# A larger pad ahead of q's pool, and one raw q buffer, in a self-attention kernel

## Chip, cores and metric

One core of a Trainium2 chip. The metric is device microseconds of one execution, the median over several executions. An interval is a 95% interval.

## The reference, cut to what matters

```python
def _L0_conv_ref(x, Wq, bq, Wk, bk, Wv, bv, gamma):      # x: (4, 64, 64, 256) float32
    q = jnp.einsum('bwhc,cd->bwhd', x, Wq) + bq           # 128 columns
    k = jnp.einsum('bwhc,cd->bwhd', x, Wk) + bk
    v = jnp.einsum('bwhc,cd->bwhd', x, Wv) + bv           # 256 columns
    pq = q.reshape(B, -1, N); pk = k.reshape(B, -1, N); pv = v.reshape(B, -1, N)   # N = 4096
    energy = jnp.einsum('bcn,bcm->bnm', pq, pk)
    attention = jax.nn.softmax(energy, axis=-1)
    out = jnp.einsum('bcm,bnm->bcn', pv, attention)
    return gamma * out.reshape(B, W, H, C) + x
```

There are four images, each with a 4096 x 4096 attention. The kernel splits operands into parts of type fp32r and forms each product from three matmuls.

## The kernel before

Per image the main loop has 128 steps, `u`, in 16 groups of eight. `t` is the step's number in its group. A step runs 12 energy matmuls on TensorE (`sa`, `sa`, `sb`, four times), and then 8 matmuls each with `vh`, `vl` and `vd`. All of them have 128x128 weights and a moving operand of 256 or 258 columns. "bb" below is the product with `vd` and `d`.

```python
xpool, xtpool, qkv = pool("xpool", 3), pool("xtpool", 3), pool("qkv", 1)

pool("pad", 1).tile([P, 16], F32, name="pad")      # 64 bytes a partition
ppool = pool("ppool", 2)                           # x, y, h, l, d
pool("pad2", 1).tile([P, 16], F32, name="pad2")    # 64 bytes: the change is here
work, kpool = pool("work", 2), pool("kpool", 3)    # work: raw q ("qr"), q, o ...; kpool: k
...
vh = qkv.tile([P, NM, VC], F32R, tag="vh", name="vh")   # VC = 260: rows of 1040 bytes
vl = qkv.tile([P, NM, VC], F32R, tag="vl", name="vl")
vd = qkv.tile([P, NM, C], F32R, tag="vd", name="vd")    # rows of 1024 bytes
...
def load_q(b, g):
    t = work.tile([P, NJ, P], F32, tag="qr", name=f"qr_{b}_{g}")
    nc.sync.dma_start(t, qd[b, g])
    loads[b, "qr", g] = t
...
# energy(b, u, k), called for k = 0 and 1
for i in range(2):
    for to, f, first, last in ((sa, 0, True, False), (sa, 1, False, True), (sb, 2, True, True)):
        nc.tensor.matmul(to[:, i], kt[:, 2 * k + i, f, :], q[:, f], start=first, stop=last)
...
# attend(b, u)
for left, right in ((h, vh), (l, vl), (d, vd)):
    for j in range(NJ):
        out_ = bb[:, j, :] if left is d else acc[j]
        for i in range(4):
            m = 2 * t + i // 2 + NI * (i % 2)
            nc.tensor.matmul(out_, left[:, i, j * P : (j + 1) * P], right[:, m, : out_.shape[1]], ...)
```

The first operand given to `matmul` is the stationary one (the weights: k, h, l, d), the second the moving one (q, vh, vl, vd).

## Time and profile before

| | before |
|---|---|
| median of the first three runs | 2494.41 us (2494.12 to 2496.48) |
| PE busy, weight loads busy | 99%, 98% |
| spacing, energy matmuls | 117 to 119 ns in most steps |
| spacing, bb matmuls | about 120 falling to 113 ns within the eight |

A *spacing* is the time from the start of one matmul to the start of the next. It is taken from the start times, in nanoseconds, that the trace holds for every matmul. The rows of the page give durations instead, and those overlap. The prediction shows the page's rows and the timeline.

### The profile page before, as it was taken

To read this page: it belongs to the slowest core of one execution; us is meant where nothing else is said; L and a number is where in the kernel's file an instruction comes from. 1 tells how busy PE (TensorE), PEld (TensorE's weight loads), DVE (VectorE), ACT (ScalarE), POOL (GpSimd) and SP (SyncE) were. 2 spreads that over 40 slices of the span, in tenths; PEclk is the share of its full clock that TensorE was granted. 3 is DMA by queue.
4 is the path that set the end of the run, shared out by engine and by line. 5 is a ranking of instruction groups with operands and counts; after the bars stand their busy time and mean duration, and the time that the engine had idled before them with its cause. 6 is when DMAs were issued, how large, how long until landed. Compare 5 with 4: busy or idle time off the path is not lost.

```text
span 2494.6 us, 50085 instructions
## 1 busy us (share of the span) xinstructions
PE 2481.1 (99%) x19982; PEld 2438.4 (98%) x19982; DVE 2106.9 (84%) x2440; ACT 1809.1 (73%) x3138; POOL 425.7 (17%) x780
## 2 busy tenths in 40 slices
PE   9999999999999999999999999999999999999998
PEld 8999999999899999999989999999998999999998
DVE  5888888888698888888869888888886988888887
ACT  5777777777677777777667777777766777777775
POOL 4211111111411111111041111111114111111110
PEclk9999999999999999999999999999999999999999
DMA  7666666664766666666477666666648666666663
GB/s 231 222 195 210 201 201 200 198 202 156 235 220 193 206 199 203 206 188 208 139 244 223 197 193 209 201 208 195 191 145 253 217 201 196 203 203 207 199 193 110
DMA packets 137408, 498.92 MB, mean 200 GB/s; under 512 B 15536, under 2 KB 57264, under 8 KB 137168
## 3 DMA queue, kind: packets, MB, share of 16 engines
q0 software_dynamic: 92320, 453.17, 58.0%
q1 hardware_dynamic: 44304, 42.22, 5.7%
q8 instruction: 160, 2.62, 0.4%
q14 instruction: 80, 0.66, 0.1%
q10 hardware_dynamic: 544, 0.26, 0.0%
HBM read 445.25 MB, written 50.33 MB: 199 GB/s over the span
## 4 chain that ended last, share of the span: by engine, by line
PE 95%; ACT 2%; DVE 1%; issue 1%; DMA 1%; POOL 0%; SPq 0%; ACTq 0%; DVEq 0%; POOLq 0%
PE a L370 38%; PE sa L320 19%; PE bb L370 18%; PE sb L320 10%; PE qk L136 4%; PE v L157 4%; PE ot L416 1%; PE xt L123 1%; ACT h L339 1%; DVE x L334 1%; ACT x L324 0%; ACT y L324 0%; ACT vh L284 0%; DMA kf<-f 0%; DVE vd L287 0%
## 5 line engine op out<-in xcount | busy, mean ns | idle before, releaser
L324 ACT ACTIVATE x<-sa 128x512 f32<-128x512 f32 x1024 | 609.4, 595 | 398.3 <-PE sa L320 330.0
L320 PE MATMUL sa<-q,k 128*128 128x256 f32 x4096 | 757.4, 283 | 1.4 <-ACT x L324 0.9
L334 DVE TENSOR_TENSOR x<-x,y 128x1024 f32<-128x1024 f32 x512 | 625.9, 1222 | 155.6 <-ACT y L324 155.6
L320 PEld LDWEIGHTS sa<-q,k 128*128 128x128 f32 x4096 | 625.7, 189 | 2.8 <-ACT x L324 1.7
L345 DVE TENSOR_TENSOR l<-x,h 128x1024 fp32r<-128x1024 f32 x512 | 624.6, 1220 | 0.0
L348 DVE SCALAR_TENSOR_TENSOR d<-h,x 128x1024 fp32r<-128x1024 f32 x512 | 624.5, 1220 | 0.0
L324 ACT ACTIVATE y<-sb 128x512 f32<-128x512 f32 x1024 | 613.2, 599 | 0.0
L320 PE MATMUL sb<-q,k 128*128 128x256 f32 x2048 | 582.0, 284 | 0.0
L370 PE MATMUL a<-vh,h 128*128 128x258 f32 x4096 | 578.3, 284 | 0.0
L339 ACT ACTIVATE h<-x 128x1024 fp32r<-128x1024 f32 x512 | 543.7, 1062 | 43.1 <-DVE x L334 38.3
L370 PE MATMUL a<-vl,l 128*128 128x258 f32 x4096 | 573.3, 282 | 0.0
L370 PE MATMUL bb<-vd,d 128*128 128x256 f32 x4096 | 557.3, 278 | 0.0
L304 POOL DMA_DIRECT2D k<-kf x512 | 280.5, 548 | 1485.6 <-PE sb L320 1467.0
L370 PEld LDWEIGHTS a<-vh,h 128*128 128x128 f32 x4096 | 526.3, 190 | 0.0
L370 PEld LDWEIGHTS a<-vl,l 128*128 128x128 f32 x4096 | 526.2, 190 | 0.0
L370 PEld LDWEIGHTS bb<-vd,d 128*128 128x128 f32 x4096 | 514.1, 188 | 0.0
L320 PEld LDWEIGHTS sb<-q,k 128*128 128x128 f32 x2048 | 384.5, 188 | 9.4 <-ACT y L324 1.4
L136 PE MATMUL qk<-wqk_sb,xts 128*128 128x256 f32 x512 | 122.8, 383 | 0.0
L400 DVE SCALAR_TENSOR_TENSOR o<-a,o 128x256 f32<-128x256 f32 x126 | 47.6, 420 | 86.9 <-ACT o L380 86.9
L157 PE MATMUL v<-xts,wv_sb 128*128 128x256 f32 x512 | 120.3, 379 | 0.0
L157 PEld LDWEIGHTS v<-xts,wv_sb 128*128 128x128 f32 x512 | 97.3, 190 | 13.2
L408 ACT ACTIVATE o<-o,r 128x256 f32<-128x256 f32 x126 | 57.6, 505 | 72.4 <-DVE r L391 72.4
(54 smaller groups left out, 931.0 us busy)
## 6 DMA issues: line engine op xcount, KB each, us to landing
k<-kf POOLq DMA_DIRECT2D x512, 768.0 KB, 4.8
x<-in_x_dram SPq DMA_DIRECT2D x128, 256.0 KB, 3.6
kf<-f POOLq DMA_DIRECT2D x64, 384.0 KB, 3.8
out_dram<-x POOLq DMA_DIRECT2D x63, 256.0 KB, 2.5
qd<-qks POOLq DMA_DIRECT2D x128, 64.0 KB, 3.0
qr<-qd SPq DMA_DIRECT2D x64, 128.0 KB, 3.0
wv_sb<-in_L_conv_Wv_dram POOLq DMA_DIRECT2D x1, 256.0 KB, 5.7
out_dram<-x SPq DMA_DIRECT2D x1, 256.0 KB, 4.1
```

The lines of the kernel that those rows point to most:

```text
L136: nc.tensor.matmul(qk[:, s, :], self.xt[i][:, k, s, :], wqk_sb[:, k, :], start=(k == 0), stop=(k == KC - 1),)
L157: nc.tensor.matmul(vp[:, eh, :], wv_sb[:, k, eh * P : (eh + 1) * P], self.xt[i][:, k].rearrange("p s a -> p (s a)"), start=(k == 0), stop= ...
L304: nc.gpsimd.dma_start(t.rearrange("p (i s) f d -> p i s (f d)", s=2), kf[b, u % NU])
L320: nc.tensor.matmul(to[:, i], kt[:, 2 * k + i, f, :], q[:, f], start=first, stop=last)
L324: nc.scalar.activation(to[:, 2 * k : 2 * k + 2, :], sp.rearrange("p i j d -> p i (j d)"), AF.Exp, scale=scale,)
L334: nc.vector.tensor_tensor(x, x, y, ALU.mult)
L339: nc.scalar.activation(h, units[b, u], AF.Identity, scale=UPPER)
L345: nc.vector.tensor_tensor(l, x, h.bitcast(F32), ALU.subtract)
L348: nc.vector.scalar_tensor_tensor(d, h.bitcast(F32), 1.0 + E, x, ALU.mult, ALU.subtract)
L370: nc.tensor.matmul(out_, left[:, i, j * P : (j + 1) * P], right[:, m, : out_.shape[1]], start=(t == i == 0 and (left is h or left is d and ...
L400: nc.vector.scalar_tensor_tensor(o[:, j, :], a[:, :C], 1.0 + E, o[:, j, :], ALU.mult, ALU.add)
L408: nc.scalar.activation(o[:, j, :], o[:, j, :], AF.Identity, scale=r[:, j : j + 1])
```

## The change

The pad ahead of q's pool grows from 64 to 448 bytes. Everything after it moves, and q and k come to lie where vd and d lie, modulo 512 bytes: q goes from 416 to 288, k from 480 to 352 (vd is at 288, d at 352). SBUF was full, so the raw q tile loses its second buffer to make room.

```diff
-        pool("pad2", 1).tile([P, 16], F32, name="pad2")
+        pool("pad2", 1).tile([P, 112], F32, name="pad2")
@@
-            t = work.tile([P, NJ, P], F32, tag="qr", name=f"qr_{b}_{g}")
+            t = work.tile([P, NJ, P], F32, tag="qr", name=f"qr_{b}_{g}", bufs=1)
```

No instruction is added, removed or reordered.

## The prediction

> **What bounds the kernel now.** I read the page first, then the timeline of TensorE inside the main loop, and then the start time of every matmul in the trace, which the page's means hide.
>
> The head of the page and three rows of its table of groups (the columns are busy us and the mean ns of one):
>
> ```profile
> PE 2481.1 (99%) x19982; PEld 2438.4 (98%) x19982; DVE 2106.9 (84%) x2440; ACT 1809.1 (73%) x3138; POOL 425.7 (17%) x780
> ...
> L320 PE MATMUL sa<-q,k 128*128 128x256 f32 x4096 | 757.4, 283 | 1.4 <-ACT x L324 0.9
> L320 PE MATMUL sb<-q,k 128*128 128x256 f32 x2048 | 582.0, 284 | 0.0
> L370 PE MATMUL bb<-vd,d 128*128 128x256 f32 x4096 | 557.3, 278 | 0.0
> ```
>
> PE and the weight loads beside it are busy 99% and 98% at full clock, and PE idles almost nowhere: the span is a sum of matmul spacings. The mean of 283 ns is a latency (matmuls are pipelined). What counts is the spacing from one start to the next. Though all three rows have one shape (128x128 weights, 256 columns), bb's duration is 5 ns shorter. The timeline of PE over one step of the loop (a step is 12 energy matmuls "sa, sa, sb", then 8 with vh, 8 with vl and 8 with vd):
>
> ```profile
> 857.95 1.09 PE L370 MATMUL bb<-vd,d 128*128 128x256 f32 x8
> 858.88 0.40 PE L320 MATMUL sa<-q,k 128*128 128x256 f32 x2
> ...
> 860.29 0.89 PE L370 MATMUL a<-vh,h 128*128 128x258 f32 x6
> ```
>
> From 858.88 to 860.29 is 1.41 us for 12 energy matmuls, 117.5 ns each; from 857.95 to 858.88 is 0.93 us for 8 bb matmuls, 116 ns each. In one other kind of step the same 12 take less:
>
> ```profile
> 841.86 0.40 PE L320 MATMUL sa<-q,k 128*128 128x256 f32 x2
> ...
> 843.24 0.53 PE L370 MATMUL a<-vh,h 128*128 128x258 f32 x3
> ```
>
> That is 1.38 us, or 115 ns. With the nanosecond starts I sorted spacings by position in the step and by t, the step's number within its group of eight (t = 0 to 7; 64 groups). In the ordinary steps:
> - Energy, t = 3 to 7: 117, 119, 117, 118, ... and a last 122 or 123: 1418 ns for twelve.
> - Energy, t = 2: 118, 117, 117, 119, 116, 114, then 113 six times: 1382 ns.
> - bb, t = 0 and 2 to 7: starts between 118 and 124 and within four or five matmuls settles at 113. bb at t = 1 does not: it stays at 117 to 118.
> - vh and vl, whose tiles move by 16 bytes modulo 512 from one to the next: 113 to 130, mean about 120.
>
> So the same work has **two rhythms, 113.4 and 117.7 ns**, and holds whichever it is in. Of 1431 bb matmuls that followed a spacing of 113 or 114, 1428 had 113 or 114 again; among energy matmuls 117 and 118 lead to 117 to 119 in all but a few of 3248. The addresses in the built program say why two loops behave alike: vd (moving) lies at 288 modulo 512 and d (stationary) at 352; q lies at 416 and k at 480. Both pairs are 64 apart. In going from bb to energy both addresses jump by 128, and there the fast rhythm is lost (113 becomes 117) in t = 3 to 7, while for t = 2 the jump from the slow rhythm of bb happens to end in the fast one.
>
> **What the Trainium skill says.** "TensorE: Matmul & The Clock Gate", section Back-to-back issue gap, gives N/2.4 + 2.5 ns warm; for N = 256 that is 109.2 ns, an estimate from that page. This trace shows 113.4 at best and 117.7 commonly, so 4 to 9 ns a matmul are on top of it. The same page, Part 2, first step (LDWEIGHTS), says that PE has two independent SBUF read ports and that loading the next weights takes no bandwidth from the running matmul. The trace does not agree: only the addresses differ between 113 and 118 to 125. "SBUF — State Buffer", section on the two separate sides, says that PE does not wait on the other engines' ports. Here it agrees: with ACT idle, bb's spacing is 113.7 ns with DVE busy (528 matmuls) and 113.5 with it idle (210). Its Specifications give 224 KiB a partition, 229,376 bytes: in the built program the tiles end at 229,344 before, so a pad 384 bytes larger fits only if something goes, and that is the second raw q buffer (1,024 bytes); the end is then 228,704.
>
> **The change, part by part.** No instruction is added, removed or reordered on any engine; the built programs differ in addresses and in the waits of DMA issues on SP.
>
> (1) The pad. All of work and kpool moves; q now lies at 288 and k at 352 modulo 512, exactly as vd and d. From bb to energy nothing changes in these residues any more, and from energy to the first vh product the weights stay at 352. Energy should then inherit the rhythm that bb ended in:
> - t = 3 to 7 follow a bb at 113. 12 x 113.4 = 1361 ns for 1418: 57 ns saved a step. Such steps with all twelve energy matmuls in a row: 64 + 64 + 60 + 60 + 60 = 308. 308 x 57 = **17.6 us saved.**
> - t = 2 follows the slow bb of t = 1 and loses its lucky jump: 1418 for 1382, 36 ns x 64 = **2.3 us lost.**
> - t = 0 gains nothing. Its first vh product waits for the accumulator, which is freed by a chain from the end of bb:
>
> ```profile
> 832.82 0.59 ACT L380 COPY o<-bb 128x512 f32<-128x512 f32 x1 [0.65 <-PE bb L370]
> ...
> 833.43 0.76 DVE L400 SCALAR_TENSOR_TENSOR o<-a,o 128x256 f32<-128x256 f32 x2 [1.38 <-ACT o L380]
> ...
> 834.03 1.18 PE L370 MATMUL a<-vh,h 128*128 128x258 f32 x8
> ```
>
> The copy of bb, then the first of two DVE operations (half of 0.76), ends near 833.82; the first vh weights load at 833.97, 58 ns late, and the first spacing is 172 in place of about 117. Faster energy lengthens this wait by what it saves.
> - t = 1 gains nothing before its ninth energy matmul: two spacings of about 220 stand there, 200 ns over the usual, and the matmul starts just after ACT's y has ended (838.35), in a row of ACT work that has run back to back since DVE's r. Same reason.
>
> (2) What follows energy. vh and vl start from another rhythm than before. Their spacings depend on the running phase and on what came before, so they can move either way: I take their mean as unchanged. But bb may now settle otherwise for some t. If it stays slow for one t, then 57 ns of energy and about 20 of bb are lost in some 61 steps, 4.7 us. Before, one t in eight was slow; I count a fifth of the five slots, 5 x 0.2 x 4.7 = 4.7 us. Against that, bb of t = 1 may become fast: 57 + 25 ns in 64 steps, 5.2 us, at 0.4 that is 2.1. Net **2.6 us lost**.
>
> (3) One raw q buffer. load_q now waits for the halving of the group before. A group's load is issued two steps before its halving, so it is issued six steps after the last one, about 25 us, while a load lands in 3.0 us (at most 5.5) and has two steps, 8.5 us. From the third load of the first image on, loads waited for an old halving anyway. Cost: nothing.
>
> Sum: 2494.4 - 17.6 + 2.3 + 2.6 = 2481.7, say **2482 us**.
>
> **The rivals.**
> - *The spacing belongs to the operation, not the address* (energy changes PSUM tile and form with each matmul, bb does not). Then nothing moves: 2494. For it: energy runs at 117.7 in seven kinds of step of eight. Against it: at t = 2 the same alternation runs at 113.
> - *Other engines take it up.* DVE has three operations of 1.22 us in a step of 4.25, ACT about 3.4 us, so an ordinary step has 0.5 us in hand; only t = 0 and 1 lack it, and they are counted as zero. If the shorter steps pushed that limit into t = 2 as well, a third of the gain would go: 2487.
> - *bb falls into the slow rhythm for most t.* Then energy inherits 117.7, and bb itself loses some 20 ns a step: 2495 to 2503. Against it: in nearly all contexts seen, whatever stood before, bb ended at 113; t = 1 is the exception.
> - *bb of t = 1 becomes fast and all others stay:* 2494.4 - 17.6 - 2.9 = 2474.
>
> **Range and chances.** The best rival gives 2474, two or three bad slots give 2489 and the first rival 2494. Runs spread 2.4 us. I take 2473 to 2491. Two per cent is 49.9 us; even all 6144 energy matmuls at 4.3 ns less would give 26, so faster by over 2% has 0.01. Slower by 2% would need 4 ns on nearly every product: 0.02.
>
> **What would show it.** In the changed kernel's profile the sa and sb rows should fall from 283 and 284 towards bb's 278; twelve energy matmuls at t = 3 to 7 should take 1.36 us in the timeline; bb should stay near 278; the wait at t = 0 should grow by some 50 ns; qr's rows should show no new idle time of PE or DVE. If sa and sb stay at 283, the address idea falls. If they fall but a<-vh, a<-vl or bb rise, the gain went into other rhythms.

## The result, and the profile after

| | before | after |
|---|---|---|
| median | 2495.38 us (2494.12 to 2496.48, 4 runs) | 2483.40 us (2478.62 to 2484.47, 4 runs) |
| ratio | | 0.9948 (0.9931 to 0.9966) |

A ratio is the mean time of one kernel's runs over that of the other's of the same rounds, so it is not quite the ratio of the medians. The gain is half a per cent, clear of the noise and small.

The page of the changed kernel, its head and the rows of the five products in the loop:

```profile
PE 2463.2 (99%) x19982; PEld 2419.1 (98%) x19982; DVE 2103.2 (85%) x2440; ACT 1807.9 (73%) x3138; POOL 424.4 (17%) x780
...
L320 PE MATMUL sa<-q,k 128*128 128x256 f32 x4096 | 740.2, 279 | 1.2 <-ACT x L324 1.1
...
L370 PE MATMUL a<-vh,h 128*128 128x258 f32 x4096 | 579.8, 284 | 0.0
...
L320 PE MATMUL sb<-q,k 128*128 128x256 f32 x2048 | 574.3, 280 | 0.0
L370 PE MATMUL a<-vl,l 128*128 128x258 f32 x4096 | 573.8, 282 | 0.0
L370 PE MATMUL bb<-vd,d 128*128 128x256 f32 x4096 | 557.2, 278 | 0.0
```

sa and sb fell from 283 and 284 ns to 279 and 280. The other three products stand still within 1.5 us, and every engine's count of instructions is the same. The timeline of PE around the energy matmuls of a step with t = 6:

```profile
851.35 1.09 PE L370 MATMUL bb<-vd,d 128*128 128x256 f32 x8
852.28 0.39 PE L320 MATMUL sa<-q,k 128*128 128x256 f32 x2
...
853.53 0.28 PE L320 MATMUL sb<-q,k 128*128 128x256 f32 x1
853.64 0.53 PE L370 MATMUL a<-vh,h 128*128 128x258 f32 x3
```

From 852.28 to 853.64 is 1.36 us for twelve, 113 ns each, where it was 1.41 to 1.42 before. Summed over the whole trace, the spacings of each product are (us):

| | energy | vh | vl | bb | span |
|---|---|---|---|---|---|
| before | 747.4 | 494.9 | 489.8 | 475.4 | 2494.6 |
| after, first trace | 729.1 | 496.4 | 490.7 | 475.0 | 2476.8 |
| after, second trace (after_again below) | 733.0 | 495.2 | 490.5 | 476.3 | 2480.6 |

The gain is in energy: 18.3 us where the span fell by 17.8 in the first trace, and 14.4 for 14.0 in the second. The traced execution of the kernel before (2496.42 us) is one of its slower ones, and both traced executions of the changed kernel lie below its median, so these differences are larger than that of the medians.

By t, the median of the twelve spacings together, in ns (ordinary steps; in brackets the rhythm of the eight bb matmuls ahead):

| t | before | after, first trace | after, second trace |
|---|---|---|---|
| 0 | 1413 (fast) | 1392 (fast) | 1392 (fast) |
| 2 | 1382 (slow) | 1360 (fast) | 1413 (slow) |
| 3 | 1418 (fast) | 1360 (fast) | 1360 (fast) |
| 4 | 1418 (fast) | 1413 (slow) | 1413 (slow) |
| 5, 6, 7 | 1418 (fast) | 1360 (fast) | 1360 (fast) |

The step t = 0 shows what the wait for the accumulator did. Timeline of the changed kernel there:

```profile
860.68 0.39 PE L320 MATMUL sa<-q,k 128*128 128x256 f32 x2
860.88 0.59 ACT L380 COPY o<-bb 128x512 f32<-128x512 f32 x1 [0.63 <-PE bb L370]
...
861.50 0.76 DVE L400 SCALAR_TENSOR_TENSOR o<-a,o 128x256 f32<-128x256 f32 x2 [1.38 <-ACT o L380]
...
862.07 0.72 PE L370 MATMUL a<-vh,h 128*128 128x258 f32 x4
```

The chain from the end of bb over ACT's copy to DVE sets 862.07. Energy is at 113 ns, but its last spacing is now 145 (118 before) and the first vh spacing 194 (172 before). These waits grew by 49 ns, which is all that energy saved there.

### The profile page after: what moved, and what is told of

Read it like the earlier page. It is cut to its first block, busy times and chain, and to the rows that moved or that the text cites.

```text
span 2476.8 us, 50085 instructions
## 1 busy us (share of the span) xinstructions
PE 2463.2 (99%) x19982; PEld 2419.1 (98%) x19982; DVE 2103.2 (85%) x2440; ACT 1807.9 (73%) x3138; POOL 424.4 (17%) x780
## 4 chain that ended last, share of the span: by engine, by line
PE 95%; ACT 2%; DVE 1%; issue 1%; DMA 1%; POOL 0%; SPq 0%; ACTq 0%; DVEq 0%; POOLq 0%
PE a L370 39%; PE bb L370 19%; PE sa L320 18%; PE sb L320 10%; PE qk L136 4%; PE v L157 4%; PE ot L416 1%; PE xt L123 1%; ACT h L339 1%; DVE x L334 1%; ACT x L324 0%; ACT y L324 0%; ACT vh L284 0%; DVE vd L287 0%; DMA kf<-f 0%
## 5 line engine op out<-in xcount | busy, mean ns | idle before, releaser
L320 PE MATMUL sa<-q,k 128*128 128x256 f32 x4096 | 740.2, 279 | 1.2 <-ACT x L324 1.1
L320 PE MATMUL sb<-q,k 128*128 128x256 f32 x2048 | 574.3, 280 | 0.0
```

## The experiments

All twelve kernels gave correct results. Each edit is against the changed kernel unless it says otherwise. A step is counted as fast where its later spacings are below 115.5 ns on average. The counts of rhythm cover the 436 steps in which twelve energy matmuls follow directly on bb.

### The changed kernel again (after_again)

No edit. 

> The changed kernel once more, unedited. Theory (energy inherits the rhythm that bb ended in): 0.995 of before, twelve energy matmuls at 113 ns in the steps that follow a bb ending at 113, and the same split by t in the trace as in the first trace (slow only at t = 4, after the slow bb of t = 3). If the 6 us spread of its four timed runs comes from the rhythm, a second trace will show another set of slow t than the first; if the set is the same and the span differs, the spread has another source.

Measured: 2480.23 us (2478.15 to 2482.34), ratio 0.9935 (0.9919 to 0.9952). The profiled execution took 2482.34 us, that of the first trace 2478.62. In rhythm the two differ in one place: at t = 2 energy was slow in 6 of 64 steps in the first trace and in 61 of 64 in the second, each time after a slow bb at t = 1. At 53 ns a step (1413 less 1360) that is 2.9 of the 3.7 us. bb's own sum is 1.3 us larger. So the spread between these two executions is the rhythm of bb at t = 1. In that step energy stops for ACT, and the rhythm afterwards is not the same in every execution. Whether the timed runs without a trace spread for the same reason is not shown, and it cannot be all of it: in the second trace all but three steps at t = 2 were slow already, and runs of the changed kernel reach 2484.47 us, 2.1 us more.

### One buffer alone (one_buffer)

Against the kernel before:

```diff
-            t = work.tile([P, NJ, P], F32, tag="qr", name=f"qr_{b}_{g}")
+            t = work.tile([P, NJ, P], F32, tag="qr", name=f"qr_{b}_{g}", bufs=1)
```

> The kernel before with raw q in one buffer and the pad left at 64 bytes: q stays at 416 and k at 480 modulo 512. Theory: 2494 to 2496 us, ratio 1.000 +- 0.001, energy at 117 to 118 ns in t = 3 to 7 as before. Rival (the single buffer itself is what gained, or costs): anything outside 0.998 to 1.002.

Measured: 2495.84 us, ratio 0.9998 (0.9981 to 1.0015). Its page has the energy row of the kernel before:

```profile
L320 PE MATMUL sa<-q,k 128*128 128x256 f32 x4096 | 757.4, 283 | 0.8 <-ACT x L324 0.8
```

The single buffer costs nothing measurable and gains nothing. It only makes room.

### Everything moved by 128 bytes (shift_all)

```diff
+        pool("pad0", 1).tile([P, 32], F32, name="pad0")
         xpool, xtpool, qkv = pool("xpool", 3), pool("xtpool", 3), pool("qkv", 1)
```

> The changed kernel with 128 bytes more ahead of all tiles of the main loop, so that q and k lie at 416 and 480 modulo 512, just as in the kernel before, but vd and d lie at 416 and 480 too. Theory (what matters is that the residues do not change from bb to energy): as fast as the changed kernel, 0.993 to 0.997 of before, energy at 113 in most t. Rival (288 and 352 are good places in themselves, 416 and 480 bad ones): energy at 117 to 118, ratio near 1.000 or above, and bb slow as well.

Measured: 2483.27 us, ratio 0.9948 (0.9931 to 0.9964). Here q and k stand at 416 and 480 modulo 512, as in the kernel before, and energy is at 113 ns all the same:

```profile
L321 PE MATMUL sa<-q,k 128*128 128x256 f32 x4096 | 742.5, 280 | 1.2 <-ACT x L325 1.2
...
L321 PE MATMUL sb<-q,k 128*128 128x256 f32 x2048 | 576.1, 281 | 0.0
```

By t the rhythms are those of the second trace (at t = 2, 54 of 64 steps slow). So 288 and 352 are not good, nor 416 and 480 bad, in themselves. What counts is that q and k stand to each other, and to vd and d, as they do.

### Other distances of k from q (scan_a, scan_b, scan_c)

Each of the two q buffers and three k buffers gets its own pool, with pads between them (in scan_b and scan_c also an offset of 16 bytes inside the tile). One run then holds six distances. The core of scan_a's edit:

```diff
+        qpools = [pool("q0", 1)]
+        pool("padq", 1).tile([P, 8], F32, name="padq")
+        qpools.append(pool("q1", 1))
+        kpools = []
+        for i, n in enumerate((0, 32, 32)):
+            if n:
+                pool(f"padk{i}", 1).tile([P, n], F32, name=f"padk{i}")
+            kpools.append(pool(f"k{i}", 1))
@@
-            t = work.tile([P, 3, NJ, P], F32R, tag="q", name=f"q_{b}_{g}")
+            t = qpools[g % 2].tile([P, 3, NJ, P], F32R, tag="q", name=f"q_{b}_{g}", bufs=1)
@@
-                t = kpool.tile([P, 4, 3, P], F32R, tag="k", name=f"k_{b}_{u}")
+                t = kpools[u % 3].tile([P, 4, 3, P], F32R, tag="k", name=f"k_{b}_{u}", bufs=1)
```

> Measures the cost of a pair of residues by itself: in the changed kernel each of the two q buffers and each of the three k buffers gets its own place, so that the distance of k from q modulo 512 takes six values in one run: 0, 32, 128, 160, 256 and 288 (q at 288 or 320, k at 320, 448 or 64). Theory (the spacing is set by where the weight load of the next matmul stands against the moving read): each distance has its own steady spacing within the twelve matmuls, between 113 and 125 ns, differing by several ns. Rival (only a change of residues from one product to the next costs): after three or four matmuls all six settle at 113 to 114. Time as a whole: 2490 to 2510, as energy no longer matches bb.

> As scan_a, with the distances 48, 96, 144, 176, 192 and 224 modulo 256. Theory: each has its own steady pattern of spacings between 113 and 125 ns; if one settles at or below 113 from every entry, it is a better place for both pairs (bb and energy) than 64.[...]

> As scan_a, with the distances 16, 80, 112, 176, 208 and 240 modulo 256. Same expectations as scan_b; 176 stands in both and should give the same pattern in both, though q and k themselves lie elsewhere.

Measured: 2502.38, 2493.76 and 2501.20 us, one run each. Median of the twelve energy spacings together, in ns, by the distance of k from q modulo 256 (t = 2 to 7; 64 is from the traces above):

| 0 | 16 | 32 | 48 | 64 | 80 | 96 | 112 |
|---|---|---|---|---|---|---|---|
| 1435 | 1410 | 1426 | 1428 | 1360 or 1413 | 1435 | 1442 | 1417 |

| 128 | 144 | 160 | 176 | 192 | 208 | 224 | 240 |
|---|---|---|---|---|---|---|---|
| 1427 | 1411 | 1430 | 1415 | 1360 | 1420 | 1396 | 1426 |

So the distance matters, and the spread is 82 ns in twelve matmuls. But a value of this table is not the price of a distance alone. The jump from vd and d changes with the distance, and the entry counts too: at 96 a step took 1442 ns after a fast bb and 1408 after a slow one, and at 240 it took 1427 and 1400. The rival, that only a change of residue costs, falls: at distance 0 the spacing stays at 120 ns to the end. Two further readings matter later. Distances 0 and 256 gave the same spacings one by one (117, then 120 ten times, then 118), and so did 32 and 288 within 1 ns. 176 also agreed, with k's buffer in another place. This points to a period of 256 bytes, not 512. And 192 ran at 113 from its first matmul on, in all its 60 steps. A step at 192 and one at 144 (at t = 0) in the timeline of scan_b:

```profile
839.73 0.39 PE L328 MATMUL sa<-q,k 128*128 128x256 f32 x2
...
841.09 0.40 PE L378 MATMUL a<-vh,h 128*128 128x258 f32 x2
```

```profile
865.24 0.40 PE L328 MATMUL sa<-q,k 128*128 128x256 f32 x2
...
866.65 0.34 PE L378 MATMUL a<-vh,h 128*128 128x258 f32 x1
```

From energy to the first vh product it is 1.36 us in the first and 1.41 in the second, with the same instructions.

### 256 bytes less pad (pad_192)

```diff
-        pool("pad2", 1).tile([P, 112], F32, name="pad2")
+        pool("pad2", 1).tile([P, 48], F32, name="pad2")
```

> The changed kernel with a pad of 192 bytes in place of 448: q at 32 and k at 96 modulo 512, which is 256 away from vd and d, the same modulo 256. In scan_a the distances 0 and 256, and 32 and 288, gave the same spacings one by one. Theory (the residues count modulo 256): as fast as the changed kernel, 0.993 to 0.996, energy at 113 in t = 0, 3, 5, 6, 7. Rival (modulo 512, as the change has it): the jump of 256 between bb and energy loses the rhythm, energy at 117 to 118, ratio 0.998 to 1.002.

Measured: 2483.41 us, ratio 0.9957 (0.9941 to 0.9974). Energy is 1360 ns in the same t as in the first trace. The residues count modulo 256, and the change's 512 asks for more than is needed.

### 32 bytes more (jump_32)

```diff
-        pool("pad2", 1).tile([P, 112], F32, name="pad2")
+        pool("pad2", 1).tile([P, 120], F32, name="pad2")
```

> The changed kernel with a pad of 480 bytes: q at 320 and k at 384, still 64 apart, but both 32 further on than vd and d. Theory (the jump from bb to energy decides): energy no longer inherits bb's rhythm; it falls in either rhythm by where the jump lands it, the same way in all steps that come from a bb at 113; in the more likely case at 117.7, and then 2490 to 2497 us; first energy spacings differ from 113. Rival (only the distance of 64 counts, and q near vd): as the changed kernel, 2480 to 2484.

Measured: 2496.49 us, ratio 1.0006 (0.9989 to 1.0023). The distance from q to k is 64 as in the changed kernel and both stand 32 bytes away from vd and d. The whole gain is gone:

```profile
L320 PE MATMUL sa<-q,k 128*128 128x256 f32 x4096 | 757.6, 283 | 1.1 <-ACT x L324 0.8
...
L320 PE MATMUL sb<-q,k 128*128 128x256 f32 x2048 | 581.5, 284 | 0.0
...
L370 PE MATMUL bb<-vd,d 128*128 128x256 f32 x4096 | 559.5, 279 | 0.0
```

The counts of the step from bb to energy show what the jump does:

| steps, bb's end to energy's end | fast to fast | fast to slow | slow to fast | slow to slow |
|---|---|---|---|---|
| before (jump of 128 in both) | 0 | 374 | 62 | 0 |
| jump_32 (jump of 32 in both) | 0 | 367 | 69 | 0 |
| after, first trace (no jump) | 362 | 4 | 0 | 70 |
| pad_192 (no jump modulo 256) | 363 | 4 | 0 | 69 |

With either of these two jumps, of both operands together, the rhythm turns over without exception: a fast bb gives a slow energy and a slow bb a fast one. Without a jump it is kept in all but four steps. The place itself does not forbid the fast rhythm: 69 steps of jump_32 ran fast at 320 and 384.

### Distance 192 for both pairs, for energy alone, for bb alone (both_192, e_192, bb_192)

The scan suggested that 192 knows the fast rhythm alone. If so, both pairs should stand there. both_192:

```diff
-        pool("pad", 1).tile([P, 16], F32, name="pad")
+        pool("pad", 1).tile([P, 48], F32, name="pad")
@@
-        pool("pad2", 1).tile([P, 112], F32, name="pad2")
-        work, kpool = pool("work", 2), pool("kpool", 3)
+        pool("pad2", 1).tile([P, 16], F32, name="pad2")
+        work = pool("work", 2)
+        pool("pad3", 1).tile([P, 32], F32, name="pad3")
+        kpool = pool("kpool", 3)
```

e_192 has pad3 alone, and bb_192 the two edits of pad and pad2 alone. The larger pad moves h and l together with d, so in both_192 and bb_192 the vh and vl products stand at another distance too.

> In scan_b the distance 192 held 113 ns from the first energy matmul on in all its steps, also where it was entered by a jump. Here both pairs lie 192 apart: d and k at 192 past vd and q modulo 256, with vd and q in the same residue. Theory: only the fast rhythm exists at this distance. bb settles at 113 at once (mean 113.5 for 116), which is 8 x 2.5 ns x 512 = 10 us, and energy is 113 in t = 2 and 4 as well, 53 ns x 124 = 6.6 us, less what t = 0 and 1 lose to their waits (about 2): 2466 to 2471 us, 0.988 to 0.991 of before. Rival (113 held in the scan by the luck of its entries): 2478 to 2486 as the changed kernel.

> The changed kernel with 128 bytes between q's pool and k's: q at 288 as vd, k at 480, so that energy is at distance 192 and no longer matches bb, which stays at 64. Theory (192 has only the fast rhythm): energy at 113 in every t, also t = 4 after the slow bb of t = 3; bb as before: 2475 to 2481. If matching bb were needed, energy would fall out as in jump_32: 2490 or more.

> Only bb at distance 192, energy left at 64 and entered by a jump of k's residue. Theory: bb at 113 from its first or second matmul in every t, mean 113.5 to 114; energy in either rhythm, the same in all t as all enter from the same rhythm: 2470 to 2475 if fast, 2484 to 2490 if slow.

Measured: both_192 2501.88 us, ratio 1.0028 (1.0012 to 1.0045); e_192 2481.84, 0.9947 (0.9930 to 0.9964); bb_192 2489.89, 0.9978 (0.9962 to 0.9995).

both_192 is slower than the kernel before, and my expectation missed by more than 30 us. The timeline of PE in one of its steps, t = 5:

```profile
855.28 0.40 PE L322 MATMUL sa<-q,k 128*128 128x256 f32 x2
...
856.70 1.10 PE L372 MATMUL a<-vh,h 128*128 128x258 f32 x8
857.64 1.11 PE L372 MATMUL a<-vl,l 128*128 128x258 f32 x8
858.58 1.11 PE L372 MATMUL bb<-vd,d 128*128 128x256 f32 x8
859.53 0.40 PE L322 MATMUL sa<-q,k 128*128 128x256 f32 x2
```

Energy takes 1.42 us, 118 ns each, and bb 0.95, 119 each. In this kernel bb at 192 has the slow rhythm too, and it does not leave it: in seven of eight t its spacings stay at 117 to 118 to the end, where at 64 they fall to 113. Energy, matched, then inherits the slow rhythm: 379 steps slow to slow and 57 fast to fast, none that changes. In scan_b the 60 steps at 192 had all followed a fast bb, and I took their inheritance for a property of the distance. e_192 says the same with the other sign. There energy at 192 follows bb at 64 and keeps its rhythm (305 fast to fast, 127 slow to slow, 4 fast to slow), though k stands 128 further on than d. The theory had t = 4 fast and 2475 to 2481 us; t = 4 stayed slow.

In bb_192 d stands 128 further on than k, and bb is slow in seven of eight t (481.7 us in sum for 476.3 in after_again), where the theory had it at 113. The time fell within the upper of the two ranges expected, but for another reason: energy is mostly fast (730.6 us). There a difference of 128 in the weights alone does not keep the rhythm: 60 of 60 fast entries stayed fast, but of 376 slow ones 282 turned fast and 94 stayed slow. What a jump of one operand does is thus not settled.

So matching is not what gains. A matched energy takes over what bb hands it, and the change gains because bb at distance 64 finds the fast rhythm in most steps. Why bb does not find it at 192 is open: its distance changed, and so did what vh and vl hand it.

### Longer rows of vh (both_192_vh)

both_192 with `vh` of rows of `VC + 4` values, 1056 bytes:

```diff
-        vh = qkv.tile([P, NM, VC], F32R, tag="vh", name="vh")
+        vh = qkv.tile([P, NM, VC + 4], F32R, tag="vh", name="vh")
```

> both_192 with vh's rows 16 bytes longer (1056 for 1040 bytes), so that the phases of the vh products move by 32 and not 16 bytes modulo 256. The constant distances that are multiples of 32 measured 117.0 ns on average in the scans (120, 118, 115, 119, 119, 120, 113, 117), the others about 118.5. Theory: the vh products change by 0 to 2 ns each, a change of -6 to +3 us against both_192; the rest as there.

Measured: 2504.91 us, ratio 1.0038 (1.0022 to 1.0055). The vh products took 493.5 us for 494.2 in both_192, and bb 2 us more. (The mean of the eight spacings that the expectation lists is 117.6 ns, not 117.0.) Nothing gained; and as it stands on both_192, it does not tell what it would do on the changed kernel. No version here beats the changed kernel clearly: e_192 and pad_192 are level with it.

## Why the prediction was right

**The mechanism held.** It said that one shape of matmul has two rhythms, that a jump of the residues between bb and energy loses the fast one, and that equal residues hand it on. The turning over in the kernel before and jump_32, against the keeping in the changed kernel and pad_192, shows it. shift_all rules out that the new places themselves are what gains, and one_buffer that the buffer is. The first rival (the spacing belongs to the operation) falls by the table by t. The third (bb slow for most t, 2495 to 2503 us) did not come here, but it is what both_192 then did, at 2501.88. One thing the prediction took for chance is regular: it said that the jump at t = 2 "happens to end" in the fast rhythm, and behind a slow bb it did so in 62 of 62 steps, and in 69 of 69 of jump_32.

**t = 3 to 7, 17.6 us.** Four of the five came as said: at t = 3, 5, 6 and 7 energy went from 1418 to 1360 ns, 58 for 57. Over 240 steps (244 less four at t = 5 that stayed slow) that is 13.9 us. t = 4 stayed slow (1413), because bb at t = 3 now ends slow.

**That a slot would fall out** was in part (2), as a fifth of five slots at 4.7 us: one slot did. bb at t = 3 itself went from 925 to 948 ns for its eight, 23 ns where "about 20" was said.

**t = 2, a loss of 2.3 us.** Right in the second trace (1413 for 1382 in 61 of 64 steps) and wrong in the first, where bb at t = 1 was fast in 58 of 64 steps and energy took 1360. The 0.4 given to that case was fair, but it is settled anew in each execution, which the prediction did not foresee.

**t = 0 and 1, nothing.** Right at t = 0, and the wait grew by 49 ns for "some 50". At t = 1 the two long spacings stayed (219 and 223 before, 213 and 222 after).

**vh and vl, unchanged in the mean.** Right within 1.5 and 0.9 us.

**The raw q buffer, nothing.** Right, by one_buffer.

The sum: 2482 was said and 2483.40 measured. Of the forecast gain of 12.4 us, 12.0 came (2495.38 less 2483.40). Partly that is luck: the lost slot and the lucky one at t = 2 nearly balance in the first trace. And the four runs behind 2483.40 lie up to 5.9 us apart; the four of after_again have a median of 2480.23. The parts are a better test of the prediction than the sum.

**What stays open.** The trace holds when each matmul and weight load starts. It does not show why two address distances cost differently, or why vh and vl hand bb one rhythm or the other. A collision of the two reads is the natural reading, and it was only argued: where the prediction says that the trace does not agree with the skill on the weight load's bandwidth, the runs show that spacing depends on addresses, and no more. No experiment reached inside.

## What to carry to other kernels

When TensorE is busy 99% of the span, look at the start-to-start spacing of matmuls of one shape, by position in the loop: if it falls into distinct values, the placement of operands is worth trying, and a pad adds no instruction (here it cost the room of one buffer). Keep residues modulo 256 equal from one product to the next where both can run fast, and check which rhythm the earlier product hands on before matching anything to it. A placement seen to be fast in one context must be tried behind a slow predecessor before it is trusted.

## What the Trainium skill lacked or had wrong

- "TensorE: Matmul & The Clock Gate", section Back-to-back issue gap: the gap has no term for operand addresses. For 256 columns its formula, which the section gives for an isolated matmul, comes to 109.2 ns (an estimate), and its figures for streams of weight loads and matmuls are for 128 and 512 columns; constant distances between weights and moving operand ran between 113.3 ns (1360 / 12) and 120.2 ns (1442 / 12) here.
- The same page, Part 2, step on LDWEIGHTS: it says that loading the next weights takes nothing from the running matmul. It does not say that spacing depends on where weights and moving operand stand. Here twelve matmuls of the same shapes took 1360 ns (changed kernel) or 1414 (jump_32, q and k moved together by 32 bytes), and at every other distance of k from q except 192 the median lay between 1396 and 1442 ns. Whether the weight load is what takes the time, and the page so wrong, no run shows.
- "SBUF — State Buffer": no rule on where two operands of one matmul should stand to each other. The period measured here is 256 bytes: the distances 0 and 256 gave equal spacings, and 192 bytes of pad served as well as 448 (2483.41 and 2483.40 us).
- No page has it: at a distance of 64 bytes a stream of equal matmuls can hold one of two rhythms, 113.4 or 117.7 ns. In the changed kernel, where the residues do not change, 362 of 366 fast entries stayed fast and 70 of 70 slow ones slow over twelve matmuls.
